# First step of an image: input tiles copied inside SBUF, column image written through GpSimd's queue

## The chip, the cores and the metric

The kernel runs on one core of one Trainium2 chip. A core has a matrix engine (TensorE, PE), a vector engine (VectorE, DVE), a scalar engine (ScalarE, ACT), a general engine (GpSimd, POOL) and an engine that issues transfers (SyncE, SP). Each takes its own instructions in order; they meet at semaphores. Transfers between DRAM and the on-chip memory (SBUF) run on 16 DMA engines. Matmul results are written to a second on-chip memory, PSUM. The metric is the time of one execution on the device in microseconds (us).

## The reference

The input is a batch of two images, 96 channels by 128 by 128. What is computed, cut to its core:

```python
# layer 0
x = x + mamba4(ln_c(x))          # four directions: rows, rows reversed, columns, columns reversed
t = t + ffn0(ln_t(t))            # with fp8 and fp16 rounding
# layer 1
x = x + conv3x3(ln_c(x))
t = t + ffn1(ln_t(t))

def mamba(x, ...):               # per direction, L = 16384 positions, 192 channels, 16 states
    xc, z = split(x @ in_w.T)
    xc = silu(causal_conv4(xc) + conv_b)
    dt, B, C = split(xc @ xproj_w.T);  dt = softplus(dt @ dt_w.T + dt_b)
    h = exp(dt * A) * h + dt * B * xc          # a scan over the positions
    y = (h . C + D * xc) * silu(z)
    return y @ outp_w.T
```

The row direction reads the normalized image as it lies in memory, the column direction reads it transposed, position by position down each column.

## The kernel before

The images are worked on one after the other: `normalize`, `mamba`, `ffn_and_conv`. The order of the instructions on each engine is written out by hand (`in_order`): each engine runs them as the code issues them.

`normalize` makes the layer norm of the image in 32 tiles of 512 positions (`layernorm`, L121) into one SBUF tile xn of 96 partitions by 16384. Each four tiles are written to DRAM as xnr (L174, SP's queue). After the last tile, VectorE copies xn column by column into staging buffers stg of 8 columns each (L184), three buffers taken in turn, and each is written to DRAM as the column image xnc (L185, SP's queue): 16 copies, 16 writes. xn leaves SBUF when this stage ends, and the tiles of the next stage take its place.

`mamba` runs 64 steps of 512 positions: 32 forward (rows and columns together), then 32 reversed. A step works on 3 groups of 128 channels (row channels, a mixed group, column channels). The loop goes over units: 24 in a step, one for each group and pair of states. In each unit ScalarE makes two decays (L351), VectorE runs two scans (L355) and a product (L450), GpSimd makes the inputs of the scans (L341) and some of the products (L362), and TensorE sums over the states in PSUM (L359).

What comes before a step's scans is the prologue (L216): load the input tiles xa (rows) and xb (columns); for each group, in the order 1, 0, 2, the convolution (`conv`, TensorE, four taps) and its way out of PSUM (`conv_out`, ScalarE); the gate z (`gate`, `gate_out`); SiLU; the matmul for B, C and dt (`rows`, L268), a round trip through DRAM that spreads these rows over the partitions (`rows_to_dram` L279, `row_tile` L337); softplus. Each item of the prologue has a unit and a place within it (0 before the scans, 1 after) at which it is issued. For later steps these units lie in the step before, so the prologue runs beside scans. For the first step of an image, all items up to unit 23 are issued at once, ahead of the first scan; items with a higher number fall into the step's own units (24 is its unit 0).

Three narrow places of the prologue matter here. All its matmuls write the one PSUM buffer misc, so each waits until ScalarE has emptied the one before. Group 1 goes through a single SBUF buffer, mix, from which two transfers spread it to its place in xc (L258, SP's queue); the gate of group 1 uses mix too. And in an image's first step xa and xb are loaded through GpSimd's queue (L228), xb after the first piece of the column image is in DRAM. Tiles of pools that are closed leave their SBUF to the pools opened next, and an instruction that writes a new tile waits for the last users of what lay there.

Of the kernel before, what the change touches and what calls it, by code (L numbers as in the profile page):

```python
# [10 lines left out]
F32 = mybir.dt.float32  # L11
# [9 lines left out]
C = 96  # L21
W = 128
L = W * W
T = 512
NT = L // T
R = T // W
# [17 lines left out]
def tile_metaformer(ctx: ExitStack, tc: tile.TileContext, a: dict, out: bass.AP):  # L44
    nc = tc.nc
# [5 lines left out]
    def const(name, shape):  # L51
        t = cpool.tile(list(shape), F32, name=name)
        nc.sync.dma_start(t, a[name])
        return t
# [8 lines left out]
    acc = accp.tile([C, L], F32, name="acc")  # L63
    blk = 4 * T

    def read(b, acc, j):

        nc.sync.dma_start(acc[:, bass.ts(j, blk)], a["x"][b, :, bass.ts(j, blk)])
# [5 lines left out]
    inz = const("inz", (C, 4, DI))  # L74
# [46 lines left out]
    def layernorm(x, eps, dst, wp, psp, bufs=2, **cast):  # L121

        xm = psp.tile([C, T], F32, name="xm", bufs=bufs)
        nc.tensor.matmul(xm, center, x, start=True, stop=True)  # L124
        yield
        sq = wp.tile([C, T], F32, name="sq")
        nc.scalar.activation(sq, xm, AF.Square)
        yield
        v = psp.tile([C, T], F32, name="v")
        nc.tensor.matmul(v, mean_w, sq, start=True, stop=True)  # L130
        yield
        rs = wp.tile([C, T], F32, name="rs")
        nc.scalar.activation(rs, v, AF.Ln, bias=eps)
        nc.scalar.activation(rs, rs, AF.Exp, scale=-0.5)
        yield
        if len(dst.shape) == 3:
            xm, rs = (t.rearrange("c (h w) -> c h w", w=W) for t in (xm, rs))
        nc.vector.tensor_tensor(dst, xm, rs, ALU.mult, **cast)

    def together(*streams):  # L140

        turn = 0
        streams, done = list(streams), object()
        while streams:
            left = []
            for at, g in streams:
                if turn < at or next(g, done) is not done:
                    left.append((at, g))
            streams = left
            turn += 1  # L150

    def in_order(st):

        et = mybir.EngineType
        st.enter_context(tc.manual_schedule(engines={et.Activation, et.DVE, et.Pool, et.PE, et.SP}))

    def normalize(b, acc, xnr, xnc):

        with ExitStack() as st:
            pool = lambda n, bufs, **kw: st.enter_context(tc.tile_pool(name=n, bufs=bufs, **kw))  # L160
            wp, psp = pool("n2", 3), pool("n_ps", 2, space=PSUM)
            in_order(st)
            nc.scalar.preload_act_table_set("natural_log_exp_and_others")
            full = pool("n1", 1)
            xn = full.tile([C, L], F32, name="xn")
            if b > 0:
                read(b, acc, L // blk - 1)

            def one(r):
                sl = bass.ts(r, T)  # L170
                yield from layernorm(acc[:, sl], eps_c[0:C, 0:1], xn[:, sl], wp, psp, 5)
                if (r + 1) % 4 == 0:
                    sl = bass.ts(r // 4, blk)
                    nc.sync.dma_start(xnr[:, sl], xn[:, sl])  # L174

            streams = [(r, one(r)) for r in range(NT)]
            with ExitStack() as weights:
                together(*streams, *([(0, prep(weights))] if b == 0 else []))
            stg = pool("n3", 3)
            cols = xn.rearrange("c (h w) -> c w h", w=W)  # L180
            part = 8
            for j in range(W // part):
                t = stg.tile([C, part, W], F32, name="stg")
                nc.vector.tensor_copy(t, cols[:, bass.ts(j, part), :])  # L184
                nc.sync.dma_start(xnc[:, bass.ts(j, part * W)], t.rearrange("c w h -> c (w h)"))  # L185

    def mamba(acc, xnr, xnc):

        with ExitStack() as st:
            pool = lambda n, bufs, **kw: st.enter_context(tc.tile_pool(name=n, bufs=bufs, **kw))  # L190

            io, gen, one, mixp, two = (pool(*p) for p in (("io", 2), ("gen", 4), ("one", 1), ("mixp", 1), ("two", 2)))
            ps_w, ps_y, ps_m = (pool(n, k, space=PSUM) for n, k in (("ps_w", 3), ("ps_y", 1), ("ps_m", 1)))
            rows_d = pool("rows_d", 3, space=DRAM)

# [4 lines left out]
            def misc():  # L200
                return ps_m.tile([128, T], F32, name="misc")

            def inproj(pi, g, w, src, taps):

                ps = misc()
                for k in taps:
                    se = {"start": k == taps[0], "stop": k == taps[-1]}
                    for d, rows, lo, hi in (
                        ((0, slice(0, 128), 0, 128),),
                        ((0, slice(0, 64), 128, 192), (1, slice(64, 128), 0, 64)),  # L210
                        ((1, slice(0, 128), 64, 192),),
                    )[g]:
                        nc.tensor.matmul(ps[rows, :], w(PAIRS[pi][d], k, lo, hi), src[d][:, k : k + T], **se)  # L213
                return ps

            def prologue(pi, i, d):  # L216

                rev = pi == 1
                lo = L - (i + 1) * T if rev else i * T
                src = []  # L220

                def load():
                    for n, dram in (("xa", xnr), ("xb", xnc)):
                        t = io.tile([C, T + 3], F32, name=n)
                        if i == 0:
                            nc.gpsimd.memset(t[:, T : T + 3] if rev else t[:, 0:3], 0.0)
                            queue = nc.sync if rev else nc.gpsimd
                            queue.dma_start(t[:, 0:T] if rev else t[:, 3 : T + 3], dram[:, lo : lo + T])  # L228
                        else:
                            nc.sync.dma_start(t, dram[:, lo : lo + T + 3] if rev else dram[:, lo - 3 : lo + T])  # L230
                        src.append(t[:, ::-1] if rev else t)
                    d["dtu"], d["yg"] = [], []
# [8 lines left out]
                    nc.scalar.activation(t, d["ps"], AF.Identity, bias=convb[:, pi, g : g + 1])  # L241

                def gate(g):
                    d["ps"] = inproj(pi, g, lambda dd, k, lo, hi: inz[:, dd, lo:hi], src, (3,))

                def gate_out(g):
                    if g == 1:
                        d["sz"] = two.tile([128, NG, T], F32, name="sz")
                    nc.scalar.copy(mixed("sz") if g == 1 else d["sz"][:, g, :], d["ps"])  # L249

                def mixed(name):
                    d["mix", name] = mixp.tile([128, T], F32, name="mix")
                    return d["mix", name]
# [54 lines left out]

                first = pi == 0 and i == 0
                at = [(-3, 1, load), (3, 0, partial(mix, "xc")), (11, 0, partial(silu, "xc"))]  # L310
                at += [(9, 0, partial(mix, "sz")), (31, 1, partial(silu, "sz"))]
                at += [(12, 0, rows), (13, 1, rows_out), (14, 0, rows_to_dram)]
                for g, k in ((1, 1), (0, 5), (2, 9)):
                    at += [(k, 0, partial(conv, g)), (k + 1, 1, partial(conv_out, g))]
                for g, k in ((1, 7), (0, 18), (2, 21)):
                    at += [(k, 0, partial(gate, g)), (k + 1, 0, partial(gate_out, g))]
                soft = ((0, 1, 16), (1, 3, 26)) if first else ((0, 3, 17),)
                for x0, x1, k in soft:
                    at += [(k, 1, partial(softplus, x0, x1))]
# [2 lines left out]
                for g, k in enumerate((19, 27, 29)):  # L322
                    at += [(k, 0, partial(dt_u, g))]
                    if i > 0:
                        at += [((20, 24, 29)[g], 1, partial(entry, g))]

                outs = (conv_out, gate_out, rows_out, dt_out)
                at = [(k, where, getattr(f, "func", f) not in outs, f) for k, where, f in at]
                return sorted(at, key=lambda p: p[:3])
# [69 lines left out]
            for k, where, rank, f in prologue(*steps[0], state[0]):  # L399
                if k < nu:  # L400
                    f()
                else:
                    later(k - nu, where, rank, f)
# [73 lines left out]
            for k in range(total + 6):  # L477
                n, u = divmod(k, nu)
# [7 lines left out]
                if k < total:  # L486
                    (g, s) = units[u]
                    da, b = das.pop(k), bs.pop(k)
# [149 lines left out]
    for b in range(NB):  # L638
        xnr = dpool.tile([C, L], F32, name="xnr")
        xnc = dpool.tile([C, L], F32, name="xnc")  # L640
        normalize(b, acc, xnr, xnc)
        mamba(acc, xnr, xnc)
        ffn_and_conv(b, acc)


# [69 lines left out]
```

## Time and profile before

| | us |
|---|---|
| median of 3 runs (11278.91 to 11287.82) | 11283.08 |
| the profiled execution | 11287.49 |
| its span | 11285.7 |
| busy: VectorE, TensorE, GpSimd, ScalarE | 10543.8, 10324.5, 9810.1, 7902.4 |
| granted TensorE clock, mean | 0.984 |
| first image: last normalized tile ends, first scan starts | 68.5, 128.7 |
| second image: the same | 5702.0, 5763.2 |
| in between, first image: VectorE busy, from 68.5 to 99.1 and from 99.1 to 128.7 | 16.27, 0.00 |

Times within the profile are counted from the span's start. A row of the timeline has the start, the duration, the engine, the line of the code, the operation and its tiles, and in brackets how long the engine had idled before it and what ended that. The chain that ended last is the way back from the last instruction, at each step to what released it. A DMA instruction in a queue's row (SPq, POOL) is the issue; the transfer's landing is told apart.

### The profile page before, as it was taken

How to read it: one execution, taken by the hardware profiler on the slowest of the kernel's cores; microseconds unless marked ns; L12 is line 12 of the kernel's file. 1: busy time of each engine (PE TensorE's matmuls, PEld its weight loads, DVE VectorE, ACT ScalarE, POOL GpSimd, SP SyncE). 2: the span in 40 equal slices, each digit the busy share in tenths (PEclk: the TensorE clock that was granted, in tenths of full speed). 3: DMA queues.
4: the chain of work that ended last, by engine and by line, in shares of the span. 5: the costliest groups of instructions: out<-in, count | busy, mean ns of one | idle time of the engine just before them, and what ended most of it. 6: DMA issues, size and time to landing. Idle time of an engine off the chain costs nothing.

```text
span 11285.7 us, 94221 instructions
## 1 busy us (share of the span) xinstructions
PE 10324.5 (91%) x24592; PEld 4019.4 (36%) x24592; DVE 10543.8 (93%) x10333; ACT 7902.4 (70%) x13564; POOL 9810.1 (87%) x4912
## 2 busy tenths in 40 slices
PE   8999999999999999988889999999999999999888
PEld 2333333333333333334433333333333333333344
DVE  6999999999999999995569999999999999999955
ACT  6777777777777777765567777777777777777655
POOL 5999999999999999992259999999999999999922
PEclk9999999999999999998989999999999999999988
DMA  7888888888888888880078888888888888888700
GB/s 278 344 337 339 342 340 341 337 340 340 337 340 341 338 338 345 336 319 18 27 261 342 339 337 344 337 337 344 337 340 342 340 342 336 340 342 336 312 13 13
DMA packets 540752, 3416.96 MB, mean 303 GB/s; under 512 B 67532, under 2 KB 68652, under 8 KB 143832
## 3 DMA queue, kind: packets, MB, share of 16 engines
q1 hardware_dynamic: 539960, 3410.16, 77.5%
q8 instruction: 199, 3.26, 0.1%
q14 instruction: 337, 2.76, 0.1%
q0 software_dynamic: 256, 0.79, 0.0%
HBM read 3289.04 MB, written 54.53 MB: 296 GB/s over the span
## 4 chain that ended last, share of the span: by engine, by line
DVE 56%; issue 19%; PE 11%; ACT 10%; POOL 2%; DMA 1%; DVEq 0%; SPq 0%; POOLq 0%; ACTq 0%
DVE da L355 34%; DVE row L355 10%; DVE row L450 9%; PE y L359 4%; ACT da L351 3%; PE pc L608 3%; POOL row L362 2%; ACT sz L261 2%; ACT L261 2%; PE xm L124 2%; ACT L262 2%; PE v L130 1%; PE ph L570 1%; DVE sz L366 1%; PE po L589 1%
## 5 line engine op out<-in xcount | busy, mean ns | idle before, releaser
L341 POOL TENSOR_TENSOR row<-dtu,row 128x2048 f32<-128x2048 f32 x1536 | 6951.3, 4526 | 8.9 <-DMA row<-bcd 8.3
L359 PE MATMUL y<-row,ident 128*128 128x512 f32 x12288 | 5681.4, 602 | 370.2 <-DVE row L450 357.5
L355 DVE TENSOR_TENSOR_SCAN da<-da,row 128x512 f32<-128x512 f32 x4608 | 5498.2, 1216 | 79.0 <-POOL row L362 22.5
L351 ACT ACTIVATE da<-dt,amat 128x512 f32<-128x512 f32 x6144 | 4234.6, 691 | 176.4 <-DVE row L355 6.3
L359 PEld LDWEIGHTS y<-row,ident 128*128 128x128 f32 x12288 | 2250.0, 190 | 3679.6 <-issue 2248.2
L450 DVE TENSOR_TENSOR row<-da,row 128x1024 f32<-128x1024 f32 x2304 | 2770.6, 1202 | 0.1
L362 POOL TENSOR_TENSOR row<-row,row 128x1024 f32<-128x1024 f32 x768 | 1807.0, 2353 | 268.7 <-issue 145.3
L451 ACT COPY hst<-da 128x2 f32<-128x2 f32 x2304 | 369.5, 160 | 2296.4 <-DVE row L450 2293.5
L355 DVE TENSOR_TENSOR_SCAN row<-da,row 128x512 f32<-128x512 f32 x1536 | 1847.8, 1203 | 71.0 <-POOL row L341 71.0
L213 PE MATMUL misc<-xa,inx 96*64 96x512 f32 (+1 forms) x2048 | 940.3, 601 | 25.4 <-DMA xa<-xnr 17.4
L213 PE MATMUL misc<-xb,inx 96*64 96x512 f32 (+1 forms) x2048 | 944.4, 604 | 18.6 <-ACT mix L249 13.6
L595 POOL TENSOR_TENSOR acc<-acc,y 96x512 f32<-96x512 f32 x128 | 147.2, 1150 | 599.1 <-DVE y L594 590.1
L374 PE MATMUL misc<-acc,ident 96*96 96x512 f32 x512 | 388.2, 843 | 218.5 <-ACT hst L451 196.5
L300 POOL TENSOR_TENSOR dtu<-dt,xc 128x512 f32<-128x512 f32 x384 | 487.8, 1270 | 91.2 <-DMA xb<-xnc 86.0
L213 PEld LDWEIGHTS misc<-xa,inx 96*64 96x64 f32 (+1 forms) x2048 | 324.6, 164 | 592.5 <-issue 484.5
L456 PE MATMUL y<-xc,dmat 128*128 128x512 f32 x768 | 420.7, 629 | 110.3 <-DVE sz L366 110.3
L608 PE MATMUL pc<-seg,uw 96*96 96x256 f32 x1536 | 443.7, 402 | 50.2 <-DVE acc L614 50.2
L376 PE MATMUL misc<-sz,gmat 128*96 128x512 f32 x1024 | 483.7, 594 | 0.0
L286 PE MATMUL misc<-rows,dtw 12*128 12x512 f32 x768 | 434.1, 645 | 50.6 <-ACT dt L291 37.9
L213 PEld LDWEIGHTS misc<-xb,inx 96*64 96x64 f32 (+1 forms) x2048 | 326.4, 164 | 279.5 <-issue 203.3
L345 POOL TENSOR_TENSOR row<-row,enter 128x4 f32<-128x4 f32 x1488 | 298.2, 200 | 116.6
L608 PEld LDWEIGHTS pc<-seg,uw 96*96 96x96 f32 x1536 | 259.0, 172 | 317.9 <-issue 178.4
(90 smaller groups left out, 7599.3 us busy)
## 6 DMA issues: line engine op xcount, KB each, us to landing
row<-bcd SPq DMA_DIRECT2D x3072, 1024.0 KB, 7.4
xc<-mix SPq DMA_DIRECT2D x256, 128.0 KB, 4.8
sz<-mix SPq DMA_DIRECT2D x256, 128.0 KB, 4.9
xa<-xnr SPq DMA_DIRECT2D x124, 193.1 KB, 5.2
xb<-xnc SPq DMA_DIRECT2D x124, 193.1 KB, 5.5
bcd<-rows SPq DMA_DIRECT2D x128, 128.0 KB, 4.3
acc<-in_x_dram SPq DMA_DIRECT2D x16, 768.0 KB, 5.8
xnr<-xn SPq DMA_DIRECT2D x16, 768.0 KB, 4.3
```

Source lines behind the costliest of these rows:

```text
L213: nc.tensor.matmul(ps[rows, :], w(PAIRS[pi][d], k, lo, hi), src[d][:, k : k + T], **se)
L261: nc.scalar.activation(d[name], d[name], AF.Silu)
L286: nc.tensor.matmul(d["ps"], w, d["rows"][0 : 2 * RK, :], start=True, stop=True)
L300: nc.gpsimd.tensor_tensor(dtu, d["dt"][:, g, :], d["xc"][:, g, :], ALU.mult)
L341: nc.gpsimd.tensor_tensor(b, d["dtu"][g][:, None, :].broadcast_to((128, 4, T)), b, ALU.mult)
L351: nc.scalar.activation(da[:, j, :], d["dt"][:, g, :], AF.Exp, scale=amat[:, pi, g, s + j : s + j + 1])
L355: nc.vector.tensor_tensor_scan(h[:, j, :], da[:, j, :], b[:, j, :], 0.0, ALU.mult, ALU.add)
L359: nc.tensor.matmul(y, ident, c[:, j, :], start=False, stop=s + j == S - 1)
L362: nc.gpsimd.tensor_tensor(c, h, c, ALU.mult)
L376: nc.tensor.matmul(d["po"], gmat[:, pi, 2 * g - 2 + k, :], d["yg"][g - 1 + k], start=False, stop=k == 1)
L450: nc.vector.tensor_tensor(c, h, c, ALU.mult)
L608: nc.tensor.matmul(pc[:, k, :], uw[:, k, ky, :], rows, start=ky == 0, stop=ky == 2)
```

## The change

In an image's first forward step, xa and xb are no longer loaded from DRAM. The pool io is opened ahead of `normalize`, two tiles of it (`heads`) are filled there by two VectorE copies from xn, rows 0 to 511 and the first four columns, with a GpSimd memset of the three leading zeros, and `mamba` takes these tiles. The 16 writes of the column image go through GpSimd's queue in place of SP's. In the first step the three gates move from units 7/8, 18/19, 21/22 to 24, 27 and 28, that is to units 0, 3 and 4 beside the scans, each matmul at place 0 and its copy at place 1 of the same unit; the spreading transfers of the gate's mix move from unit 9 to 25. Since pairs of gate and gate_out may now lie across another item, the gate's PSUM tile has a name of its own in the bookkeeping (`pz`). The pool of misc is as before.

```diff
@@ normalize
+            for t, first in zip(heads, (xn[:, 0:T], cols[:, 0:R, :])):
+                nc.gpsimd.memset(t[:, 0:3], 0.0)
+                into = t[:, 3 : T + 3]
+                nc.vector.tensor_copy(into if t is heads[0] else into.rearrange("c (w h) -> c w h", h=W), first)
             part = 8
             for j in range(W // part):
                 t = stg.tile([C, part, W], F32, name="stg")
                 nc.vector.tensor_copy(t, cols[:, bass.ts(j, part), :])
-                nc.sync.dma_start(xnc[:, bass.ts(j, part * W)], t.rearrange("c w h -> c (w h)"))
+                nc.gpsimd.dma_start(xnc[:, bass.ts(j, part * W)], t.rearrange("c w h -> c (w h)"))
@@ mamba
-            io, gen, one, mixp, two = (pool(*p) for p in (("io", 2), ("gen", 4), ("one", 1), ("mixp", 1), ("two", 2)))
+            gen, one, mixp, two = (pool(*p) for p in (("gen", 4), ("one", 1), ("mixp", 1), ("two", 2)))
@@ load
+                        if i == 0 and not rev:
+                            src.append(heads[len(src)])
+                            continue
                         t = io.tile([C, T + 3], F32, name=n)
                         if i == 0:
-                            nc.gpsimd.memset(t[:, T : T + 3] if rev else t[:, 0:3], 0.0)
-                            queue = nc.sync if rev else nc.gpsimd
-                            queue.dma_start(t[:, 0:T] if rev else t[:, 3 : T + 3], dram[:, lo : lo + T])
+                            nc.gpsimd.memset(t[:, T : T + 3], 0.0)
+                            nc.sync.dma_start(t[:, 0:T], dram[:, lo : lo + T])
@@ prologue
-                at += [(9, 0, partial(mix, "sz")), (31, 1, partial(silu, "sz"))]
+                at += [(25 if first else 9, 0, partial(mix, "sz")), (31, 1, partial(silu, "sz"))]
-                for g, k in ((1, 7), (0, 18), (2, 21)):
-                    at += [(k, 0, partial(gate, g)), (k + 1, 0, partial(gate_out, g))]
+                gates = ((1, 24, 24, 1), (0, 27, 27, 1), (2, 28, 28, 1)) if first else ((1, 7, 8, 0), (0, 18, 19, 0), (2, 21, 22, 0))
+                for g, k, o, where in gates:
+                    at += [(k, 0, partial(gate, g)), (o, where, partial(gate_out, g))]
@@ for each image
-        normalize(b, acc, xnr, xnc)
-        mamba(acc, xnr, xnc)
+        with tc.tile_pool(name="io", bufs=2) as io:
+            heads = [io.tile([C, T + 3], F32, name=n) for n in ("xa", "xb")]
+            normalize(b, acc, xnr, xnc, heads)
+            mamba(acc, xnr, xnc, io, heads)
```

More of the change, by code (lines that the diff above doesn't have):

```diff
@@ L155, in in_order, with normalize @@
         st.enter_context(tc.manual_schedule(engines={et.Activation, et.DVE, et.Pool, et.PE, et.SP}))
-    def normalize(b, acc, xnr, xnc):
+    def normalize(b, acc, xnr, xnc, heads):
         with ExitStack() as st:
@@ L184, in normalize, with mamba @@
                 nc.vector.tensor_copy(t, cols[:, bass.ts(j, part), :])
-                nc.sync.dma_start(xnc[:, bass.ts(j, part * W)], t.rearrange("c w h -> c (w h)"))
-    def mamba(acc, xnr, xnc):
+                nc.gpsimd.dma_start(xnc[:, bass.ts(j, part * W)], t.rearrange("c w h -> c (w h)"))
+    def mamba(acc, xnr, xnc, io, heads):
         with ExitStack() as st:
             pool = lambda n, bufs, **kw: st.enter_context(tc.tile_pool(name=n, bufs=bufs, **kw))
-            io, gen, one, mixp, two = (pool(*p) for p in (("io", 2), ("gen", 4), ("one", 1), ("mixp", 1), ("two", 2)))
+            gen, one, mixp, two = (pool(*p) for p in (("gen", 4), ("one", 1), ("mixp", 1), ("two", 2)))
             ps_w, ps_y, ps_m = (pool(n, k, space=PSUM) for n, k in (("ps_w", 3), ("ps_y", 1), ("ps_m", 1)))
@@ L243, in gate @@
                 def gate(g):
-                    d["ps"] = inproj(pi, g, lambda dd, k, lo, hi: inz[:, dd, lo:hi], src, (3,))
+                    d["pz"] = inproj(pi, g, lambda dd, k, lo, hi: inz[:, dd, lo:hi], src, (3,))
                 def gate_out(g):
@@ L248, in gate_out @@
                         d["sz"] = two.tile([128, NG, T], F32, name="sz")
-                    nc.scalar.copy(mixed("sz") if g == 1 else d["sz"][:, g, :], d["ps"])
+                    nc.scalar.copy(mixed("sz") if g == 1 else d["sz"][:, g, :], d["pz"])
                 def mixed(name):
```

## The prediction

> **What bounds the kernel now.** I read the page first (DVE 93%, POOL 87%, PE 91% busy over the span), then the tenths over 40 slices: VectorE and GpSimd fall at the two places where an image begins. The change touches only that place, so what it is worth is read there, from the chain that ended last in order of time. For the first image, columns start, duration, what:
>
> ```profile
> 67.82 0.70 DVE xn L138
> 68.54 1.03 DVE stg L184
> 69.72 5.25 DMA xnc<-stg
> ...
> 89.92 3.54 DMA xnc<-stg
> 93.55 1.03 DVE stg L184
> 95.61 2.80 DMA xc<-mix
> 99.14 5.98 PE misc L213 x8
> 105.85 1.28 ACT L261
> 107.14 1.49 ACT xc L261
> 108.68 5.44 PE misc L268 x6
> 114.75 2.06 DMA bcd<-rows
> 116.83 7.22 DMA row<-bcd
> 124.19 4.51 POOL row L341
> 128.72 2.34 DVE row L355 x2
> ```
>
> From the last normalized tile (68.5) to the first scan (128.7) nothing runs on VectorE but the sixteen staging copies; 60 us, and as much in the second image (5702.0 to 5763.2). The first half of it is the writing of the column image, three staging buffers taken in turn. The first transfer of the step's own work, xc<-mix, stands on SP behind all sixteen writes. ScalarE shows the other end of it (timeline):
>
> ```profile
> 91.39 0.69 ACT L241 ACTIVATE xc<-misc,convb 128x512 f32<-128x512 f32 x1 [3.79 <-PE misc L213]
> 98.50 0.59 ACT L249 COPY mix<-misc 128x512 f32<-128x512 f32 x1 [6.43 <-DMA xc<-mix]
> ```
>
> The gate's copy waits until xc<-mix has emptied the one mix buffer, and the convolution of group 2 (99.14) waits for that copy, because there is one misc PSUM buffer. So both the input loads (PE begins on xb at 79.88) and the write stream stand on this road; the write stream ends last.
>
> How GpSimd issues a DMA is shown four times. Timeline of the second image, VectorE and POOL:
>
> ```profile
> 5708.77 1.04 DVE L184 COPY stg<-xn 96x1024 f32<-96x1024 f32 x1 [3.83 <-DMA xnc<-stg]
> 5708.97 0.96 POOL L228 DMA_DIRECT2D xb<-xnc  x1 [4.91 <-DMA xnc<-stg]
> ```
>
> The issue ends at 5709.93, 0.12 after the copy; in the first image the pair ends at 76.10 and 76.21. SP's issue of a write takes 0.30 (median of 32).
>
> [...] both single pairs end 0.11 and 0.12 after a copy. It shows no POOL issue without a copy beside it, and no write through that queue. [...] eight matmul passes took 5.98 after 5.94 us of idling (99.14), 3.70 after a gap of 0.78 (87.65).
>
> **The change, part by part**, on the first image's clock.
>
> *Input tiles from SBUF.* Removed: two loads through POOL, xa landing at 75.5 and xb at 79.8. Added: two VectorE copies of 512 elements, half of a 1.03 us staging copy each, 1.1 us together, ahead of the sixteen. The first convolution can start at 69.7 in place of 79.9. That alone is worth 10 us only if its consumer can run.
>
> *It can't.* The io pool now opens before the normalization, so everything above it moves up by 8,320 bytes: the staging buffers lay at bytes 174,240 to 186,528 of a partition and now lie at 182,560 to 194,848. The mix buffer stays at 189,088 to 191,136, so it now lies in the second and third staging buffer. The built program's list of waits says so: the first ACT instruction of the step (conv_out into mix) waits for VectorE's last staging copy and for all eight of the POOL queue's semaphores at the count of sixteen writes; in the kernel before it waited for the xnr writes and no column write. With one misc buffer, the convolutions of groups 0 and 2 queue behind it, and on SP xc<-mix, bcd, the next xa and xb and the row fetches. The convolution moved forward just waits in PSUM. What sets the end is T, the landing of the sixteenth column write.
>
> *T.* Before, the fourth copy (first reuse of a buffer) began at 75.07, and twelve more copies took 18.48, or 4.62 for a turn of three buffers: copy 1.03, hand-over 0.1 to 0.2, issue to landing about 3.4 (median 3.5). After, add to each turn the extra of a POOL issue, e. Issue 0.95 against 0.30 gives 0.65[...]. Neither is shown for this form, so e is bounded by 0 ([...]landing as before; less only if the missing 0.4 MB of loads shortened landings, and those loads met one turn of five) and 2.1[...]. I take 0.8: copies stand 0.3 to 0.7 apart, so some issues escape the copy. The 1.1 of head copies mostly disappears in the first landing, which was slow (5.25) behind a 768 KB xnr write: fourth copy at 75.4. Sixteenth: 75.4 + 4 x 5.42 = 97.1; its copy 1.03, issue 0.95, landing 3.4: T = 102.5.
>
> *From T to the rows matmul.* Before: group 2 starts at 99.14, rows at 108.68. After: wait and mix 0.79, PE hand-over 0.05, group 0 at cold clock 5.96 (TensorE has idled since about 78), ACT 0.79 with hand-overs, group 2 warm 3.75, then as before from the end of group 2 to rows (105.15 to 108.68) 3.53: 14.9. Rows start at 117.4, later by 8.7. The gate and its mix, no longer between groups 0 and 2, save about 8 us that are in this sum.
>
> *Second image.* Fourth copy 5708.77 + 0.35, turns of 4.73 + 0.8: sixteenth copy at 5731.2, T = 5736.6, rows 5751.5 against 5743.42: later by 8.1.
>
> *Gates in units 0 to 4.* Three gate matmul sets and 3 x 0.58 of ScalarE copies leave the stretch before the first scan, where rows fetched at 116.8 and landed at 124.1 decide: nothing gained. In units 3 and 4 the copies meet ScalarE's softplus turn: VectorE idles 1.72 there until 145.24, then 0.40 until 148.13 for POOL's product. The decay needed at 148.13 was ready at 146.54 and will be at 147.3: hidden, slack 0.8. Without that cover, 1.2 an image. On SP, sz<-mix now stands behind seven row fetches and holds two more until ScalarE has made six decays (about 124.6 on the old clock); the first of the two is used at 151.6, so this is hidden too. On POOL the sixteen writes stand ahead of the first dtu (118.65), which waits for softplus anyway.
>
> *Sum.* 8.7 + 8.1 = 16.8. The profiled execution took 11287.5 (span 11285.7, 1.8 around it) and would take 11304; the median, 4.4 lower, goes from 11283.1 to 11300.
>
> **The rivals.** What measurement can tell from no change is about 0.2%, 22.6 us, 11.3 an image.
>
> - *Each POOL issue sits out a further copy (e = 2.1).* For it: both observed issues end with a copy, and copies that run back to back leave no gap. Against: in the trace copies have gaps. Per image 4 x 1.3 for the turns and 1.0 at the end more than my sum: +29 in all, 11312. It decides, as slower, from e of about 1.4.
> - *The POOL queue costs nothing (e = 0), TensorE stays warm.* For it: without xa and xb there is less traffic, and DMA engines were busy 81% of this stretch. Per image 4 x 0.8, 0.65 and up to 2.3 less: about +4, 11287.
> - *The change does what its words say:* the early convolution runs on, the column writes are off the road. Conv to mix at 77, groups 0 and 2 to 86.6, rows at 90.1, or 18.5 earlier in each image: 11246. Against: the wait in the program. Since rows follow T by 14.9, no loss needs a T of 93.8, and a gain of 0.2% one of 82.5, thirteen copies and landings after 75.
>
> **How the numbers follow.** My case 0.67; e = 2.1 or near it 0.20; about nothing 0.10; as the words say 0.03. The likeliest gives 11300. Its own range is 11290 to 11305; the range for 8 in 10 takes in the two neighbours, 11287 to 11313, and leaves out the last. Faster by over 0.2%: 0.03; within: 0.77; slower: 0.20.
>
> **What would show it.** First convolution near 70, and the first mix activation only after 100, its wait ended by a DMA xnc<-stg from POOL's queue; POOL issues near 0.9 long; turns of three copies near 5.4; group 0 at about 5.9; first scan near 137. Wrong would be: mix before 95 (then the placement was misread), turns under 4.7 or over 6, or new stalls of VectorE in units 0 to 7.

## The result and the profile after

The changed kernel takes 11303.25 us in the median (11300.55 to 11313.22) against 11285.49 for the kernel before in the same session: 17.8 us more, a ratio of 1.0017 with a 95% interval of 1.0011 to 1.0024. Forecast were 11300 and 16.8 more. The profiled execution took 11300.55 us, its span is 11298.8 (before: 11287.49 and 11285.7).

The chain that ended last, first image of the changed kernel. Columns: start, duration, what.

```profile
68.78 0.69 DVE xn L138
...
69.72 0.73 DVE xb L184
70.45 0.99 DVE stg L188
...
72.08 4.11 DMA xnc<-stg
...
76.28 1.03 DVE stg L188
...
97.58 1.03 DVE stg L188
...
98.89 3.69 DMA xnc<-stg
...
102.84 0.70 ACT mix L247
...
103.58 6.49 PE misc L217 x8
110.10 0.70 ACT xc L247
...
110.84 3.71 PE misc L217 x8
...
118.11 4.16 PE misc L274 x6
...
122.90 2.05 DMA bcd<-rows
...
140.04 2.35 POOL row L369
```

In the kernel before, xc<-mix stood in this place behind the sixteen writes; now the mix activation itself does. (The chain passes the first scan by; that scan is the first row of VectorE's timeline below.) TensorE had the first convolution finished at about 76, and its result waited in PSUM until the sixteenth column write had landed at 102.58. ScalarE's timeline gives the wait its name and length; the second row, of the next step, matters below:

```profile
102.84 0.69 ACT L247 ACTIVATE mix<-misc,convb 128x512 f32<-128x512 f32 x1 [34.09 <-DMA xnc<-stg]
...
147.88 0.69 ACT L247 ACTIVATE mix<-misc,convb 128x512 f32<-128x512 f32 x1 [3.63 <-DMA sz<-mix]
```

In the kernel before, both of these activations waited for TensorE and for no transfer:

```profile
86.91 0.69 ACT L241 ACTIVATE mix<-misc,convb 128x512 f32<-128x512 f32 x1 [19.12 <-PE misc L213]
...
139.23 0.69 ACT L241 ACTIVATE mix<-misc,convb 128x512 f32<-128x512 f32 x1 [1.92 <-PE misc L213]
```

VectorE's timeline, at the first scan and at the first longer stall after it (unit 3). The kernel before has its first scan at 128.72, and its stall there is the last row here:

```profile
135.65 2.34 DVE L362 TENSOR_TENSOR_SCAN row<-da,row 128x512 f32<-128x512 f32 x2 [37.05 <-POOL row L348]
...
153.75 2.50 DVE L362 TENSOR_TENSOR_SCAN da<-da,row 128x512 f32<-128x512 f32 x2 [3.30 <-ACT da L358]
```

```profile
145.24 2.50 DVE L355 TENSOR_TENSOR_SCAN da<-da,row 128x512 f32<-128x512 f32 x2 [1.72 <-ACT da L351]
```

GpSimd's issues of the column writes, all 32 of them, are in the changed kernel's rows of that line (min/median/max in ns) and of their transfers:

```profile
L189 POOL DMA_DIRECT2D xnc<-stg x32: 505/507/1384, 72.1 to 5739.8; - x32
...
DMA to landing us min/median/max: 3.3/4.0/5.3
```

Single executions wander. Two stretches that no edit here touches show it: from the scan after that stall to the second image's last normalized tile, the profiled executions of this document took 5553.5 to 5563.9 us, and from the same scan of the second image to the end 5497.2 to 5507.6. A step of a few microseconds is therefore read in a window that begins where the last normalized tile of an image ends. Three marks are used: the mix activation, the first scan, and the scan after the stall in unit 3. In us after that tile, first image / second image; the last two columns sum the third mark's difference over both images, and give the difference of medians, each against the kernel before in its own session:

| kernel | mix | first scan | after the stall | sum to before | median to before |
|---|---|---|---|---|---|
| before | 18.40 / 17.28 | 60.21 / 61.21 | 76.73 / 78.18 | 0 | 0 |
| changed | 33.37 / 32.84 | 66.18 / 67.15 | 84.28 / 85.25 | +14.6 | +17.8 |
| e2_before_moved | 28.89 / 28.99 | 63.24 / 66.92 | 79.85 / 84.01 | +9.0 | +13.4 |
| e3_writes_on_sp | 28.09 / 28.35 | 60.07 / 60.68 | 77.84 / 78.89 | +1.8 | +7.3 |
| e4_gates_early | 33.20 / 33.02 | 71.41 / 71.68 | 88.06 / 88.54 | +21.7 | +17.5 |
| e8_loads | 32.84 / 33.64 | 65.96 / 67.01 | 83.75 / 85.50 | +14.3 | +12.7 |
| e9_own_stage | 33.65 / 32.71 | 65.94 / 64.67 | 83.34 / 81.64 | +10.1 | +7.2 |
| e1_place | 6.41 / 7.35 | 43.03 / 42.91 | 61.17 / 61.34 | -32.4 | -26.8 |
| e5_place_writes_on_sp | 6.47 / 7.24 | 50.36 / 50.50 | 68.32 / 68.73 | -17.9 | -17.7 |
| e7_place_loads | 16.17 / 16.44 | 46.72 / 46.57 | 64.67 / 64.57 | -25.7 | -23.5 |
| e6_place_own_stage | 6.48 / 7.25 | 43.38 / 42.16 | 59.77 / 58.27 | -36.9 | -39.5 |

The windows and the medians agree within 6 us, so the two places where an image begins carry the difference, as far as the scatter lets one say. Two cautions go with the table. The windows rest on one execution of each kernel, and they scatter too: up to the first scan the changed kernel and e9_own_stage run the same instructions, yet the second image's first scan comes at 67.15 and 64.67. Of that, 1.4 us is one convolution on TensorE, eight passes that took 6.98 us in the one and 5.54 in the other. So some 2.5 us in a mark need not come from an edit. And windows and medians don't always tell two edits apart alike: e4_gates_early lies 7.1 above the changed kernel in the windows and level with it in the medians.

TensorE's rate comes up again below. The same eight passes of a convolution took 3.70 us in many places and 5.4 to 7.1 in others; these are called the fast and the slow rate here (warm and cold in the recorded texts). The clock granted to TensorE over the passes was 1.00 where they took 3.70 (at 87.65 in the kernel before, at 110.84 and 5752.56 in the changed one), and 0.61, 0.57, 0.55 and 0.52 where they took 5.96, 6.48, 6.62 and 6.98 (99.14 before, 103.58 changed, 5733.23 before, 5744.80 changed).

### The profile page after: what moved, and what is told of

Read it like the earlier page. It is cut to its first block, busy times and chain, and to the rows that moved or that the text cites. A ratio compares the mean times of both kernels' runs of the same rounds, so it can differ in the third digit from the quotient of the medians.

```text
span 11298.8 us, 94255 instructions
## 1 busy us (share of the span) xinstructions
PE 10318.6 (91%) x24592; PEld 4020.5 (36%) x24592; DVE 10544.1 (93%) x10337; ACT 7902.6 (70%) x13564; POOL 9825.1 (87%) x4940
## 4 chain that ended last, share of the span: by engine, by line
DVE 56%; issue 19%; PE 11%; ACT 9%; POOL 3%; DMA 1%; DVEq 0%; SPq 0%; POOLq 0%; ACTq 0%
DVE da L362 33%; DVE row L362 10%; DVE row L457 9%; PE y L366 4%; PE pc L615 3%; POOL row L369 3%; ACT da L358 3%; PE xm L124 2%; ACT sz L267 2%; ACT L267 2%; ACT L268 2%; PE v L130 1%; PE ph L577 1%; DVE sz L373 1%; PE po L596 1%
## 5 line engine op out<-in xcount | busy, mean ns | idle before, releaser
L362 DVE TENSOR_TENSOR_SCAN da<-da,row 128x512 f32<-128x512 f32 x4608 | 5497.6, 1216 | 83.8 <-POOL row L369 24.2
```

The lines of the kernel that those rows point to most:

```text
L362: nc.vector.tensor_tensor_scan(h[:, j, :], da[:, j, :], b[:, j, :], 0.0, ALU.mult, ALU.add)
```

## The experiments

**The placement put right (e1_place).** Edit of the changed kernel: a gap that moves the staging buffers to the top, and a pool of its own for sz, so that what lies under them is sz alone. (In the changed kernel SP's first xc<-mix waits for xnc<-stg too, in four waits, the longest 27.7 us, so mix is not the only tile tied. As the author reads the built program's waits, the first write to any tile of a pool waits for the former users of the pool's whole area; by that, with sz left in the pool of xc and dt, xc would have waited in mix's stead. No run tries it.)

```diff
+            pool("gap", 1).tile([C, 8288], F32, name="gap")
             stg = pool("n3", 3)
...
+            szp = pool("szp", 2)
...
-                        d["sz"] = two.tile([128, NG, T], F32, name="sz")
+                        d["sz"] = szp.tile([128, NG, T], F32, name="sz")
```

> The changed kernel with one thing different: where the staging buffers lie. They are moved up to bytes 215,712 to 228,000 of a partition, under the sz buffers alone (which get a pool of their own at the same addresses), so mix, xc and dt share no byte with them. Theory (the placement's wait costs the gain): the first mix activation comes right after the convolution, at about 71, with no wait for a column write; rows matmul at about 86; the row fetches then wait only for VectorE's last staging copy at about 98, land at 105 and the first scan is near 110 in place of 135.7, so 25 us an image less than the changed kernel: about 11250, under the kernel before by about 35. Rival (the wait for the writes was not what set the end; another, the row fetches or POOL's queue, stands just behind it): first scan no earlier than 130, within 10 us of the changed kernel.

Measured: 11260.74 us (11258.92 to 11270.44), ratio to before 0.9977 [0.9967, 0.9987]. ScalarE's timeline of this kernel:

```profile
74.63 0.69 ACT L249 ACTIVATE mix<-misc,convb 128x512 f32<-128x512 f32 x1 [7.14 <-PE misc L219]
79.11 0.69 ACT L249 ACTIVATE xc<-misc,convb 128x512 f32<-128x512 f32 x1 [3.79 <-PE misc L219]
83.59 0.69 ACT L249 ACTIVATE xc<-misc,convb 128x512 f32<-128x512 f32 x1 [3.79 <-PE misc L219]
```

Its first scan, from VectorE's timeline:

```profile
111.25 2.34 DVE L364 TENSOR_TENSOR_SCAN row<-da,row 128x512 f32<-128x512 f32 x2 [14.24 <-POOL row L350]
```

The convolutions run on without a wait for a transfer. The first scan comes 23.2 and 24.2 us sooner than in the changed kernel (25 expected), and the median falls by some 43. The mix activation came at 74.6 and not at 71, because the early convolution starts at TensorE's slow rate (its first passes take 1.06 us each, the last 0.59) and lasts to 74.6. Two roads now end almost together: bcd lands at 96.2, and the row fetches wait for VectorE's last staging copy, which ends at 97.0 (by the addresses, the row buffers lie over xn, which that copy reads). Two rows of SP's queue between 60 and 130, waits by what was waited for (us in all, times, longest), show the second road, and a wait that is new:

```profile
SPq L266 <- DMA xnc<-stg: 5.2, 1, 5.2
...
SPq L346 <- DVE stg L189: 2.0, 1, 2.0
```

So the wait made by the placement was what kept the change from its gain. The rival, a first scan no earlier than 130, is out.

**The placement alone (e2_before_moved).** Edit of the kernel before:

```diff
+            pool("gap", 1).tile([C, 2080], F32, name="gap")
             wp, psp = pool("n2", 3), pool("n_ps", 2, space=PSUM)
```

> The kernel before with nothing changed but addresses: an unused 8,320 bytes ahead of the normalization's buffers, so that the staging buffers lie at 182,560 to 194,848 as in the changed kernel. Theory: the first mix activation waits for all sixteen column writes (about 98.3 in place of about 82); group 0 follows at cold clock to about 105, the gate 2 us, group 2 to 111, rows at about 114.3 in place of 108.7: +5.7 an image, +11 in all, 11296. Rival (addresses don't matter, the slower turns and the gates are the loss): no change, within 2 us of the kernel before.

Measured: 11300.87 us (11291.66 to 11309.57), ratio 1.0011 [1.0002, 1.0019]. ScalarE's timeline of this kernel:

```profile
97.04 0.69 ACT L242 ACTIVATE mix<-misc,convb 128x512 f32<-128x512 f32 x1 [29.61 <-DMA xnc<-stg]
```

With nothing moved but addresses, the mix activation takes up the wait for the column writes, 29 us after the last tile in place of 18. The first scan comes later by 3.0 in the first image (group 2 took 3.70 there) and by 5.7 in the second (group 2 took 5.40, so 1.7 of these 5.7 is TensorE's rate). The two sums, +9.0 in the windows and +13.4 in the medians, stand on either side of the 11 expected.

**The writes back on SP (e3_writes_on_sp).** Edit of the changed kernel:

```diff
-                nc.gpsimd.dma_start(xnc[:, bass.ts(j, part * W)], t.rearrange("c w h -> c (w h)"))
+                nc.sync.dma_start(xnc[:, bass.ts(j, part * W)], t.rearrange("c w h -> c (w h)"))
```

> The changed kernel with the sixteen column writes back on SP's queue, everything else left. Theory: the turn of three copies goes from 5.3 back to about 4.65 (four turns: 2.6), the last issue and landing are 0.8 shorter, so the mix activation comes 3.4 earlier in each image: about 7 us less than the changed kernel, 11296. Rival (the longer turns come from the traffic beside them, not from POOL's queue): turns stay at 5.3, no difference.

Measured: 11294.85 us (11286.67 to 11304.82), ratio 1.0006 [0.9998, 1.0015]. This kernel's rows of the writes on SP's queue, to be held against GpSimd's above:

```profile
L189 SPq DMA_DIRECT2D xnc<-stg x32: 303/304/712, 71.5 to 5735.4; - x32
...
DMA to landing us min/median/max: 2.8/3.3/4.7
```

From the fourth copy (75.82) to the sixteenth (92.86, in the chain) is 17.04, or 4.26 a turn, and 4.37 in the second image; with GpSimd's queue it is 5.33 and 5.23. The queue thus costs 1.07 and 0.86 a turn: the issue starts 0.28 after the copy's end in place of 0.02 (chain), and the transfer lands 4.0 after the start of its issue in place of 3.3, about 1.0 together; the issue itself, 0.51 against 0.30, lies within the 4.0 and the 3.3. The mix activation comes 5.3 and 4.5 sooner, more than the 3.4 expected, and group 0 runs shorter (5.63 against 6.49; in the second image 5.88 against 6.98). The shorter pause ahead of it (22 us against 27) doesn't explain that: in e9_own_stage group 0 took 5.54 after 26.1, in e2_before_moved 6.92 after 13.0. It may be chance. The rival, that the traffic alone makes the turns long, is out: at the same traffic they are shorter by 1.07 and 0.86.

**The gates early again (e4_gates_early).** Edit of the changed kernel:

```diff
-                at += [(25 if first else 9, 0, partial(mix, "sz")), (31, 1, partial(silu, "sz"))]
+                at += [(9, 0, partial(mix, "sz")), (31, 1, partial(silu, "sz"))]
-                gates = ((1, 24, 24, 1), (0, 27, 27, 1), (2, 28, 28, 1)) if first else ((1, 7, 8, 0), (0, 18, 19, 0), (2, 21, 22, 0))
+                gates = ((1, 7, 8, 0), (0, 18, 19, 0), (2, 21, 22, 0))
```

> The changed kernel with the first step's gates back in their old places ahead of the first scan, everything else left. Theory: VectorE's stall in unit 3 goes from 3.3 back to about 1.7, since the next step's mix activation no longer waits for sz<-mix behind the row fetches; against that, the gate of group 1 and its copy stand between groups 0 and 2 again, about 1.9. The two cancel: within 2 us of the changed kernel. Rival (the gates moved are worth what they took in the kernel before, some 8 us an image, because the mix buffer's emptying is waited for): 16 us slower than the changed kernel.

Measured: 11305.04 us (11290.59 to 11313.26), ratio 1.0015 [1.0009, 1.0022]: by its time not to be told from the changed kernel. The windows differ by 7.1, and show where. VectorE's timeline in unit 3, and TensorE's between the convolutions (gates are inz, convolutions inx):

```profile
157.46 2.50 DVE L362 TENSOR_TENSOR_SCAN da<-da,row 128x512 f32<-128x512 f32 x2 [1.85 <-ACT da L358]
```

```profile
110.75 0.64 PE L217 MATMUL misc<-xa,inz 96*64 96x512 f32 x1 [0.78 <-ACT xc L247]
...
112.56 7.09 PE L217 MATMUL misc<-xb,inx 96*128 96x512 f32 x8 [0.73 <-ACT mix L255]
```

The stall in unit 3 goes back from 3.30 to 1.85 (second image 3.29 to 2.06), as expected. But the first scan comes 5.2 and 4.5 later, not 1.9: the gate and its copy take 1.81 (110.75 to 112.56), and group 2 after them runs slowly, 7.09 in the first image and 5.40 in the second, in place of 3.70. In the windows, then, the move of the gates gains 4.5 to 5.2 an image ahead of the first scan, most of it TensorE's rate in the first image and 1.7 of it in the second, and gives back 1.2 to 1.5 in unit 3. The slow rate is not a single accident: with the mix activation waiting for the column writes, group 2 was slow in three of the four image starts where a gate stands between the groups (e2_before_moved and this run), and took 3.70 in all eight where none does. Why is not shown. "The two cancel" fits the medians, but not the windows; the rival's 8 an image fits neither.

**The loads in place of the copies (e8_loads).** Edit of the changed kernel:

```diff
-                into = t[:, 3 : T + 3]
-                nc.vector.tensor_copy(into if t is heads[0] else into.rearrange("c (w h) -> c w h", h=W), first)
...
+                            nc.sync.dma_start(heads[len(src)][:, 3 : T + 3], dram[:, 0:T])
                             src.append(heads[len(src)])
```

> The changed kernel, staging buffers where it has them, without the two VectorE copies into the input tiles: SP loads xa and xb of the first step from DRAM. Theory (with mix waiting for all sixteen writes, the early convolution only waits in PSUM): group 1 ends near 86 in place of 75, still 16 us ahead of the mix activation; the two loads' traffic and the 1.1 us of copies that go are about even, so the mix activation stays at 33 us after the last normalized tile, plus or minus 1.5, and the first scan at 66 to 67. Rival (the copies already pay, and the other parts lose more than was thought): first scan 5 us or more later an image.

Measured: 11301.3 us (11285.94 to 11311.25), ratio 1.001 [1.0001, 1.0019]. The mix activation comes at 32.84 and 33.64, the first scan at 65.96 and 67.01, within 0.3 of the changed kernel in both images. Under this placement the two copies are worth nothing in the windows. (The medians, each against its session, lie 5.1 apart, which the marks don't show.)

**The mix buffer left to the next step (e9_own_stage).** Edit of the changed kernel:

```diff
                 def mixed(name):
-                    d["mix", name] = mixp.tile([128, T], F32, name="mix")
+                    if name == "sz" and pi == 0 and i == 0:
+                        d["mix", name] = d["sz"][:, 0, :]
+                    else:
+                        d["mix", name] = mixp.tile([128, T], F32, name="mix")
                     return d["mix", name]
```

> The changed kernel, with the first step's gate of group 1 staged in its own sz tile in place of the mix buffer, as in e6_place_own_stage. Theory: the first scan stays at 66 to 67 us after the last normalized tile, the second step's mix activation no longer waits for sz<-mix, and VectorE's stall in unit 3 goes from 3.3 down to 1.3 to 1.8: 3 to 4 us less over the two images, 11300. Rival: the stall stays above 3.

Measured: 11295.77 us (11283.87 to 11306.59), ratio 1.0007 [1.0, 1.0013]. ScalarE's and VectorE's timelines:

```profile
145.99 0.69 ACT L247 ACTIVATE mix<-misc,convb 128x512 f32<-128x512 f32 x1 [2.79 <-PE misc L217]
```

```profile
152.00 2.50 DVE L365 TENSOR_TENSOR_SCAN da<-da,row 128x512 f32<-128x512 f32 x2 [2.59 <-ACT da L361]
```

The wait for sz<-mix is gone, but the stall falls only to 2.59 and 2.17 (1.72 and 2.16 in the kernel before). In the second image that is the whole of its growth, 1.1 us; in the first it is 0.7 of 1.6. What is late next there is the second step's convolution of group 1, nearly all of it at the slow rate: 139.14 to 145.94, 6.8 us, against 133.25 to 139.18, 5.9, in the kernel before. Neither theory had that. The edit itself accounts for about 2 us of the windows' 4.5; the other 2.5 lie ahead of the second image's first scan, where it changes nothing.

**Both repairs (e6_place_own_stage).** e1_place with the edit of e9_own_stage.

> e1_place, and the first step's gate of group 1 is staged in its own sz tile (group 0's part, which is written later) in place of the one mix buffer. Theory (the mix buffer's late release is what stalls VectorE in unit 3): the second step's mix activation no longer waits for sz<-mix, and VectorE's stall there goes from 3.3 to 3.6 down to about 1.8, as in the kernel before: 3 us less over the two images, 11257.5, hardly to be told from e1_place by its time alone. Rival (ScalarE's extra copies or PE make the stall): it stays above 3.

Measured: 11250.18 us (11247.49 to 11258.46), ratio 0.9967 [0.9955, 0.998]. VectorE's timeline of e1_place in unit 3, and then of this kernel:

```profile
129.39 2.50 DVE L364 TENSOR_TENSOR_SCAN da<-da,row 128x512 f32<-128x512 f32 x2 [3.34 <-ACT da L360]
```

```profile
128.25 2.50 DVE L367 TENSOR_TENSOR_SCAN da<-da,row 128x512 f32<-128x512 f32 x2 [1.58 <-ACT da L363]
```

Here the whole growth of the stall goes, as expected: 3.34 to 1.58, and 3.63 to 1.29 in the second image. The windows account for 4.5 us of the gain over e1_place; the rest of the 11 between their medians (and of the 10 between the profiled executions) lies in stretches that the edit doesn't touch. This version beats both kernels, by 0.33% and by about 0.5%.

**The other two parts, with the placement right.** e5_place_writes_on_sp is e1_place with e3's edit, e7_place_loads is e1_place with e8's.

> e1_place (staging buffers moved off mix, xc and dt) with the sixteen column writes back on SP's queue. Theory (once the placement is right, the queue decides): turns of three copies shrink from 5.3 to about 4.3, so the last staging copy comes about 4 us earlier; but xc<-mix stands on SP behind all sixteen writes, issued near 94 in place of 75.4 and landed at 98, so silu of xc, rows (at 100.3) and bcd follow it and the first scan comes near 121 in place of 111.3: about 20 us slower than e1_place in all, 11280. Rival (POOL's queue is only a cost): the row fetches, which wait for the last staging copy, start 4 us earlier and it is 8 us faster than e1_place, 11253.

> e1_place without the two VectorE copies into the input tiles: xa and xb of the first step are loaded from the two DRAM images by SP, as the kernel before loaded them through POOL. Theory (the copies pay once the placement lets them): convolution of group 1 ends near 86 in place of 74.6, rows near 99.5, bcd at 105, and the first scan near 119.5 in place of 111.3: 8 us an image slower than e1_place, 11277. Rival (the row fetches' wait for the last staging copy covers the loads): first scan within 2 us of e1_place, time the same.

Measured: e5 11271.93 us (11262.01 to 11279.1), ratio 0.9984 [0.9978, 0.9991], and e7 11266.11 us (11254.43 to 11278.98), ratio 0.9979 [0.9972, 0.9987]. In e5, ScalarE's table load ahead of silu shows what SP's order costs:

```profile
98.71 1.28 ACT L269 ACT_TABLE_LOAD   x1 [13.40 <-DMA xc<-mix]
```

The first scan comes 7.3 and 7.6 later than in e1_place (10 expected), although the last staging copy ends 3.4 us sooner after the last tile; in e7 it comes 3.7 and 3.7 later (8 expected). Both signs held, both sizes were too large: from the first row fetch to the first scan 11.9 was taken from the kernel before, and 10.1 and 10.7 were measured, and in e7 the rows matmul besides came 2.6 sooner after the last tile than was reckoned. So, with the placement right, both of these parts of the change pay: GpSimd's queue, a pure cost under the wrong placement, gives about 7 us an image, since xc<-mix no longer stands behind sixteen writes on SP; the copies about 3.5. The sizes are the windows'; between the medians, each against its session, they are 9.1 and 3.2 in all, and the intervals overlap. The gates were not put back under this placement.

## Why the prediction was right, and which steps were not

The sign and the size held: 16.8 us more were forecast, 17.8 measured between medians, 14.6 in the windows. The windows split the 14.6 as follows: placement +9.0 (e2); the copies nothing (e8: 0.3); the gates -7.1 (e4: 21.7 against 14.6); and GpSimd's queue +12.8 (e3: 1.8 against 14.6), of which 9.8 is the later mix activation and 2.0 group 0's passes. Summed up, 9.0 + 0.3 - 7.1 + 12.8 = 15.0. The medians, each against its session, bear out the two large terms (13.4 and 10.4), but they put 5.1 on the copies and nothing on the gates, and then the terms don't add up. So the two large terms stand in both measures; the sizes of the other two stand on single executions.

- *"It can't."* Right. Mix waited for the sixteenth write, the wait was ended by xnc<-stg, and e1 shows that it was the placement that made it: with it gone, the first scan came 23 to 24 us sooner. The rival "as the words say" put the changed kernel at 11246, 37 us less than before, if this wait were not there. In e1, which differs from the changed kernel in the placement alone, rows came 21 us earlier an image (18.5 in that rival), but the row fetches then waited for the last staging copy, and 27 us (medians) or 32 (windows) were gained over the kernel before. That e6 reached 11250 is not that rival's sum: it has a further edit.
- *T.* The sixteenth write was forecast to land 34.0 and 34.6 after the last tile; it landed after 33.1 and 32.7. The turn was right, 5.42 against 5.33 (second image 5.53 against 5.23), but by luck, as a sum of two wrong terms: issues were taken at 0.95 and were 0.51 in the median, and the queue's whole extra e was taken at 0.8, the author's estimate, on top of a turn with the two loads' traffic in it. e3 gives a turn without them of 4.26 and 4.37, and an e of 1.07 and 0.86, of which the later landing (4.0 against 3.3 from the start of the issue) is the larger part. Of these 0.7, 0.2 is the longer issue; what makes the other 0.5 is not shown. Some issues beside a VectorE copy did stretch. GpSimd's timeline of the changed kernel has one of each kind:

```profile
79.57 0.96 POOL L189 DMA_DIRECT2D xnc<-stg  x1 [1.48 <-DVE stg L188]
...
82.51 0.51 POOL L189 DMA_DIRECT2D xnc<-stg  x1 [1.29 <-DVE stg L188]
```

  The first issue starts while the copy from about 79.4 to 80.4 runs, and ends 0.11 after it; the second lies between two copies. Nine of the 32 were stretched (0.79 to 1.38), and each ended 0.11 to 0.12 after a copy. The other 23 took about 0.51. Eleven of those met a copy too, but one that began 0.28 us or more after the issue had. The rival with e = 2.1 had taken the four issues seen in the kernel before for the rule; of its 2.1, the trace carried 1.7 (0.65 of longer issue and a copy of 1.03), and the rest was not shown.
- *From T to rows.* 14.9 forecast, 15.5 and 15.9 measured: group 0 took 6.48 and 6.98 where 5.96 was taken from the kernel before (its second image had 6.62). Rows came 8.5 and 7.2 later than in the kernel before (8.7 and 8.1 forecast).
- *"Nothing gained" ahead of the first scan.* Wrong. From rows to first scan took 20.0 and 19.8 before, and 17.5 and 18.5 after. The rows matmul was 1.3 shorter in the first image (4.15 against 5.44, and 5.41 against 5.44 in the second; over all runs it took 4.1 to 5.4, so this is TensorE's rate again), and the first row fetch landed sooner after its issue by 1.3 in both (start of GpSimd's product less start of the fetch: 7.4 and 7.2 before, 6.1 and 5.8 after). The same fetch took 5.9 and 6.1 in e2, where the gates are early, so the gates are not its cause, and 5.6 to 6.7 in the other runs with the mix wait. That cause stays open.
- *"Hidden" in units 0 to 4.* Wrong. The forecast looked at ScalarE's copies and at the row fetches behind sz<-mix, and named as the price of lost cover 1.2 an image. The stall grew by 1.6 and 1.1 at the decay, and by 0.1 more at the product behind it. The step that failed was to follow sz<-mix only on SP, and not to ask who waits for the buffer it reads: mix. These are the changed kernel's transfers issued between 60 and 150 (KB each, median us to landing):

```profile
xc<-mix SPq DMA_DIRECT2D x4, 128.0 KB, 3.7
sz<-mix SPq DMA_DIRECT2D x2, 128.0 KB, 14.7
```

  Of the same size, through the same queue, sz<-mix took four times as long, because seven row fetches of 1024 KB were issued just ahead of it (and the 3.7 is itself a median of 2.3 in the first step, before the row fetches, and 5 in the second); mix came free only then, and the next step's mix activation, softplus and decay stood behind that on ScalarE. e4 and e6 take the growth of the stall away from both ends. In e9 0.9 of it stays in the first image, with TensorE.

So two misses of opposite sign, 2.5 and 1.3 gained and 1.7 and 1.3 lost, left the sum where the wait put it. That the wait set the end was understood; that the smaller misses cancelled was luck.

## What to carry to other kernels

Before an early start is counted as a gain, ask the program what the first writer of each new buffer waits for: a pool opened earlier moves every address above it, and a moved buffer can tie the first tile of the next stage to the last transfer of the stage before (in e2, where nothing else was moved, the mix activation came 29 us after the last tile in place of 17 to 18). A part of a change can then be a loss in one layout and a gain in another, as the writes on GpSimd's queue were here (in the windows 12.8 lost in the one, 14.5 gained in the other), so a layout is put right before its parts are judged. And where a small transfer moves behind large ones, follow the buffer that it reads as well as the one that it fills (sz<-mix landed after 14.7 us here, and mix was not free until then).

## What the runs showed of the hardware

- In the changed kernel a DMA issue on GpSimd took 0.505 us at its least and 0.507 in the median, up to 1.38 beside a VectorE copy of float32; SP's took 0.304 in e3. Every stretched issue (nine of 32) ended 0.11 to 0.12 us after a copy's end; an issue that began 0.28 us or more before a copy was not stretched. The same 384 KB write landed after 4.0 us through GpSimd's queue and after 3.3 through SP's.
- A 128 KB transfer behind seven fetches of 1024 KB on the same queue landed after 14.7 us; one of the same size issued before the fetches landed after 2.3.
- In e1_place, where row fetches start before the last column write is in, a column write took up to 11.0 us (5.3 at most in the changed kernel), though it is on another queue; in the first image it took 10.4, and sz<-mix on SP waited 5.2 us for that landing.
- Eight passes of a convolution took 3.70 us after a pause of 0.78, at a granted clock of 1.00 in the three listed above, and 5.5 to 7.1 after pauses of 6 to 29 us, and the longer pauses did not give the longer times (6.92 after 13.0, 5.54 after 26.1); the granted clock over four of these slow ones was 0.52 to 0.61. With the four passes of a gate between, in e2 and e4, they took 3.70 once and 5.40 to 7.09 three times after gaps of 0.8 only. What decides the rate there is not shown.
